# Layer 3 of a four-layer network: a quarter of B's products moved to GpSimd in half of the states, one ScalarE table for exp and ln, and a new schedule for a chunk's preparation

## The chip, the cores and the metric

The kernel runs on one core of a Trainium2 chip. A core has five engines with a queue each, which work side by side and wait for one another by semaphores: TensorE (in the profile PE; PEld is its weight load), VectorE (DVE), ScalarE (ACT), GpSimd (POOL) and SyncE (SP), which here only issues DMAs. The metric is the device time of one execution in microseconds, as the median of several.

## The reference

Four layers are applied one after the other to four images of 256 channels and 64 x 64 pixels, with a normalisation ahead of each: a deformable convolution (layer 0), an attention over all 4096 pixels (layer 1), a grouped deformable convolution (layer 2) and a selective state-space layer (layer 3, "mamba"). The change touches layer 3 only, which computes, for the L = 4096 pixels of an image in order:

```python
xz = einsum('bld,ed->ble', xs, in_proj_w)            # 256 -> 1024
u, res = split(xz, 2)                                 # 512 and 512 channels
u = silu(causal_conv4(u) + conv_b)
dt, Bm, Cm = split(u @ x_proj_w.T, [16, 32])          # 16, 16, 16
delta = softplus(dt @ dt_proj_w.T + dt_proj_b)        # 512 channels
state = exp(delta * A) * state + delta * Bm * u       # 512 x 16 states, along L
y = sum over the 16 states of state * Cm, + u * D
out = (y * silu(res)) @ out_proj_w.T
```

The state is a recurrence along the pixels; each of the 512 channels has 16 states, and A, Bm and Cm have one value for each of the 16.

## The kernel before

Channels lie on the 128 partitions, so 512 channels are 4 blocks of 128 (index `dc` in the code), and the pixels are cut into `NC` = 8 chunks of `C` = 512. For one image, layer 3 is a loop over 128 steps `s`: the chunk is `j = s // 16`, the state `n = s % 16`. A step does this for one state of one chunk:

- TensorE broadcasts row n of B to all partitions: a small bfloat16 matmul of `pick` with `bp` (three bfloat16 parts of B) into the one PSUM bank `bn` (L1419, in `state`).
- VectorE multiplies `du` (delta times u, 128 x 2048) by that row into the tile `h` (L1491).
- ScalarE forms `da` = exp(delta x A) block by block into two PSUM banks (L1498), and VectorE runs the recurrence over a block in place (L1499, a scan). So ScalarE can be at most two blocks ahead of VectorE.
- GpSimd keeps the last column as the start of the next chunk (`carry`, L1510) and multiplies `h` by row n of C (L1513). That row, `cn`, was broadcast to all partitions by a DMA from a small tensor `cd` in device memory (L1417, SP's queue).
- TensorE adds the four blocks of `h` of two steps ago to the four PSUM banks `y` by matmuls with the identity (L1411, in `add`). At n = 0 a matmul with a diagonal puts u x D there first (L1409). At n = 2 of the next chunk VectorE multiplies the finished y by the gate (L1468, `gated`).

A float32 matmul shows as two instructions (two passes) in the profile.

The order on TensorE, ScalarE, VectorE and GpSimd is written out by hand: each engine executes its instructions in program order. Between these instructions lies the preparation of the next chunk (`front(j)`): the normalised x (`begin`, L1245), four projections to u (L1213, copied by L1217), four convolutions of 8 passes (L1259, bias by L1264), the silu of u together with that of the last chunk's gate (L1273, L1229), the projection to dt, B and C (L1282, kept by L1286), the projection to delta with Abs and Relu (L1297, L1303, L1304), the parts of a softplus (Exp L1310, "+1" L1314, "1 - w" L1324, Ln L1326, and GpSimd's sums and products L1319, L1328 to L1330), the four gate projections (L1213 again), and the split of B into bfloat16 parts (`split`). `close(j)` projects a finished chunk to the output (L1369, L1373, copied by L1377 and sent by SP), fetches the next image's pixels and takes their statistics (`count`, L152).

Each piece has a place (step, half), and `LEAD` is how many steps ahead of its chunk the preparation begins, so that a piece of step k lies at state n = k - LEAD (negative: in the chunk before). `put(step, half, pe, rest)` enters a TensorE part and the rest. Half 0 lies between the second and the third scan, half 1 after the fourth, half 2 after the product with C, -1 after the product with B. `fill` issues the TensorE part early (that of half 0 at the end of the step before, that of half 1 ahead of the third scan), and `empty` issues the rest in its place. All these TensorE parts share one PSUM bank, "front", which is free again once ScalarE has read it.

In a step of before, TensorE's order is: the half-0 part, the half-1 part, `bn` of the next step, the eight passes of `add`. The code inserts a load of ScalarE's function table wherever the loaded set lacks the function; silu, exp and ln come from three sets, so a chunk has four loads.

## Time and profile before

| what | value |
|---|---|
| median of 3 runs | 9984.5 us (9975.76 to 9988.26) |
| the profiled execution's own time | 9981.35 us |
| its span, first to last instruction | 9979.5 us |
| granted TensorE clock, mean | 0.956 |
| layer 3's loop, first image | from 1571.69 us on, chunks of 123.08, 119.45, 119.45, 119.81, 119.45, 119.45, 118.95 us; the last to its last product 111.76 |
| the same, the other images | from 4045.13, 6517.47 and 8993.31 us on |
| a `cn` broadcast | 512 DMAs of 256 KB |

Times in the profile are in microseconds, those of single instructions in the groups in nanoseconds. A line of the groups gives: code line, engine, operation, output <- inputs with their shapes, number; then busy time in all and mean of one; then the engine's idle time just ahead of them, with what ended it. A line of a timeline gives start, length, engine, code line, operation and number of merged instructions, and in brackets how long the engine had been idle and what ended that.

### The profile page before, as it was taken

How to read it: one execution, taken by the hardware profiler on the slowest of the kernel's cores; microseconds unless marked ns; L12 is line 12 of the kernel's file. 1: busy time of each engine (PE TensorE's matmuls, PEld its weight loads, DVE VectorE, ACT ScalarE, POOL GpSimd, SP SyncE). 2: the span in 40 equal slices, each digit the busy share in tenths (PEclk: the TensorE clock that was granted, in tenths of full speed). 3: DMA queues.
4: the chain of work that ended last, by engine and by line, in shares of the span. 5: the costliest groups of instructions: out<-in, count | busy, mean ns of one | idle time of the engine just before them, and what ended most of it. 6: DMA issues, size and time to landing. Idle time of an engine off the chain costs nothing. (4 is left out here: it accounts for less than half of the span.)

```text
span 9979.5 us, 88756 instructions
## 1 busy us (share of the span) xinstructions
PE 8624.9 (86%) x29193; PEld 4231.9 (42%) x29193; DVE 7632.5 (76%) x8183; ACT 4959.9 (50%) x7576; POOL 6758.0 (68%) x3948
## 2 busy tenths in 40 slices
PE   5889998998778999899877899989977789998997
PEld 3643443333464344333346434433335643443333
DVE  4764597999676459899967646889996764679998
ACT  3743335665474332566557433266645733326664
POOL 3746786887574667688747467768875746777876
PEclk9999999999899999999989999999998999999999
DMA  7830011111793011111188201111118810111111
GB/s 264 319 138 1 31 48 38 46 45 49 258 329 113 1 34 52 36 46 45 44 293 324 82 1 40 48 40 44 45 42 313 322 63 1 42 52 34 40 41 33
DMA packets 377891, 956.56 MB, mean 96 GB/s; under 512 B 34675, under 2 KB 107820, under 8 KB 375372
## 3 DMA queue, kind: packets, MB, share of 16 engines
q0 software_dynamic: 165888, 604.05, 16.8%
q1 hardware_dynamic: 211532, 346.73, 11.1%
q8 instruction: 234, 3.83, 0.2%
q14 instruction: 237, 1.94, 0.1%
HBM read 784.59 MB, written 92.32 MB: 88 GB/s over the span
## 5 line engine op out<-in xcount | busy, mean ns | idle before, releaser
L1499 DVE TENSOR_TENSOR_SCAN h<-da,carry,h 128x512 f32<-128x512 f32 x2048 | 2470.5, 1264 | 138.3 <-ACT da L1498 89.7
L1513 POOL TENSOR_TENSOR h<-h,cn 128x2048 f32<-128x2048 f32 x508 | 2300.1, 4528 | 41.0 <-POOL carry L1510 0.2
L1498 ACT ACTIVATE da<-delta,l3a 128x512 f32<-128x512 f32 x2048 | 1389.1, 689 | 1138.6 <-DVE h L1499 1136.4
L1411 PE MATMUL y<-h,ident 128*128 128x512 f32 x4096 | 1930.8, 616 | 3.3 <-POOL h L1513 2.5
L344 POOL DMA_INDIRECT g<-tab,idx x1152 | 1355.1, 1176 | 756.7 <-issue 368.8
L565 POOL TENSOR_TENSOR acc<-acc,e 128x1024 f32<-128x1024 f32 x480 | 1125.2, 2344 | 541.6 <-ACT e L561 520.1
L388 PE MATMUL pz<-cols,l0w 128*128 128x256 f32 x4608 | 1216.2, 411 | 191.5 <-DVE cols L377 81.3
L1411 PEld LDWEIGHTS y<-h,ident 128*128 128x128 f32 x4096 | 809.8, 198 | 1295.1 <-issue 1233.3
L1491 DVE TENSOR_TENSOR h<-du,bn 128x2048 f32<-128x2048 f32 x512 | 1157.8, 2261 | 34.4 <-PE bn L1419 34.3
L353 DVE SCALAR_TENSOR_TENSOR r<-g,wx,r 128x512 f32<-128x512 f32 x1152 | 858.1, 745 | 368.2 <-ACT r L352 252.2
L462 DVE TENSOR_REDUCE m<-pm 128x3 f32<-128x1536 f32 (+2 forms) x340 | 599.3, 1763 | 699.7 <-PE pm L452 699.7
L388 PEld LDWEIGHTS pz<-cols,l0w 128*128 128x128 f32 x4608 | 896.4, 205 | 361.2 <-DVE cols L377 119.1
L561 ACT ACTIVATE e<-sc 128x1024 f32<-128x1024 f32 x512 | 496.0, 1020 | 1029.7 <-PE sc L548 1029.7
L572 PE MATMUL cx<-e,v 128*128 128x512 f32 x2048 | 1001.1, 616 | 0.0
L845 DVE TENSOR_TENSOR prod<-ring,A 128x1280 f32<-128x1280 f32 x640 | 922.6, 1480 | 79.1 <-DMA ring<-ring 60.8
L352 ACT ACTIVATE r<-g,wx 128x512 f32<-128x512 f32 x1152 | 826.4, 717 | 258.9 <-DMA g<-tab,idx 212.9
L862 PE MATMUL pacc<-prod,ident 128*128 128x512 f32 x1920 | 912.9, 609 | 35.3 <-DVE prod L845 23.3
L854 POOL TENSOR_TENSOR prod<-prod 128x512 f32<-128x512 f32 x640 | 800.1, 1274 | 184.2 <-DVE prod L845 161.6
L370 PE MATMUL pt<-ident,acc 128*128 128x128 f32 x2304 | 426.7, 294 | 297.2 <-DVE acc L361 232.9
L1510 POOL COPY carry<-h 128x4 f32<-128x4 f32 x512 | 98.0, 191 | 804.6 <-DVE h L1499 793.0
L572 PEld LDWEIGHTS cx<-e,v 128*128 128x128 f32 x2048 | 352.4, 189 | 599.1 <-issue 596.6
L360 ACT ACTIVATE acc<-r,wy 128x256 f32<-128x256 f32 x1152 | 571.9, 496 | 24.6 <-DVE r L353 22.1
(254 smaller groups left out, 10959.9 us busy)
## 6 DMA issues: line engine op xcount, KB each, us to landing
cn<-cd SPq DMA_DIRECT2D x512, 256.0 KB
tab<-vt SPq DMA_DIRECT2D x112, 640.0 KB
ring<-ring SPq DMA_DIRECT2D x288, 126.0 KB
ring<-ring SPq DMA_DIRECT2D x288, 124.0 KB
g<-tab,idx POOLq DMA_INDIRECT x1152
x<-in_x SPq DMA_DIRECT2D x64, 256.0 KB
out<-x SPq DMA_DIRECT2D x56, 256.0 KB
l0w<-in_l0w SPq DMA_DIRECT2D x4, 2304.0 KB
```

Of the source, the lines that this page charges most:

```text
L344: nc.gpsimd.indirect_dma_start(out=g[:], out_offset=None, in_=tab[:, :], in_offset=bass.IndirectOffsetOnAxis(ap=idx[:, t, k : k + 1], axis=0),
L353: nc.vector.scalar_tensor_tensor(r, g[:, :, 1, :], wx[:, 1, t, k : k + 1], r, ALU.mult, ALU.add)
L388: nc.tensor.matmul(sums[m][:, ot, :256], wf[:, i, bass.ts(ot, P)], cols[m][:, i, :], start=(i == 0), stop=(i == 17),)
L565: nc.gpsimd.tensor_add(b["acc"], b["acc"], e)
L572: nc.tensor.matmul(blocks[qb]["cx"], v[:, 4 * (i + kt // 4 * 4) + kt % 4, :], e[:, bass.ts(i % 2, 512)], start=(kt == 0 and i == 0), stop= ...
L845: nc.vector.tensor_mul(d["prod"][:, :, t, :].rearrange("p x (g c) -> p x g c", c=GC), ring[y // VR % 4][:, :, y % VR, :].rearrange("p x (g ...
L862: nc.tensor.matmul(d["pd"], self.ident, prod[:, wx, :], start=(wy == 0 and wx == 4), stop=(wy == WIN - 1 and wx == 2),)
L1411: nc.tensor.matmul(c["ys"][dc], self.ident, h[:, dc, :], start=False, stop=(n == DS - 1))
L1491: nc.vector.tensor_mul(h, c["du"], c.pop(("bn", n)).to_broadcast([P, 4, C]))
L1498: nc.scalar.activation(da, c["delta"][:, dc, :], AF.Exp, scale=al[:, dc, n : n + 1])
L1499: nc.vector.tensor_tensor_scan(h[:, dc, :], da, h[:, dc, :], carry[:, dc, n : n + 1], ALU.mult, ALU.add)
L1513: nc.gpsimd.tensor_mul(h, h, cn.to_broadcast([P, 4, C]))
```

## The change

1. **B's products.** In the states 14, 15, 0, 1, 2, 3, 4 and 5 (`helped`) VectorE multiplies three of the four blocks of `du`; GpSimd multiplies the fourth into a tile `hq` (two buffers) in the step before (`quarter(s + 1)`, between the second and the third scan), and the fourth scan reads `hq`. [...]its row of B is broadcast by a DMA into `bs` (two buffers), from `cd`, which now holds C and B. `ahead` issues both broadcasts two steps ahead; `cn` has four buffers in place of six.
2. **Order.** `bn` of the next step is issued right after the second scan, ahead of the half-1 part. At n = 2 VectorE's product of step 3 is issued there too, between the second and the third scan, ahead of `empty(s, 0)` with the silu.
3. **One table.** `tables()` loads the set that has both exp and ln after the silus, so that neither Ln nor the exp after it needs a load.
4. **The preparation.** `LEAD` becomes 5 (3 in place of 2 for the first). Projections to u go to n = 11, 12, 13 and 15, all in half 1 (they were at 12/1, 13/0, 13/1 and 14/0); convolutions to 13/0, 14/1, 0/1 and 1/1 (14/1, 15/1, 0/1, 1/1); "1 - w" from 8/0 to 8/1; the gates from 10/0 to 11/1 to 9/0 to 10/1; the output projections from 7/1 and 9/1 to 6/1 and 7/1; the statistics for most chunks from n = 9 to n = 2, half 0. The silu stays at 2/0, the shares at 3/1, delta at 4 and 5, Exp at 6/0, Ln at 9/0, and GpSimd's sums where they were.
5. **Tiles.** `kept` takes the buffer of `xn3`; `tiny`, whose exp loaded a table in `first`, goes.

```diff
-        NC, LEAD = N // C, 4
+        NC, LEAD = N // C, 5
...
-            kept = pa.tile([P, 2, C], F32, tag="kept", name="kept")
-            tiny = pa.tile([P, 1], F32, tag="tiny", name="tiny")
...
+            def tables():
+
+                nc.scalar.preload_act_table_set("natural_log_exp_and_others")
...
-                nc.scalar.activation(tiny, self.eps, AF.Exp)
+                tables()
...
-                c["cd"] = self.dram.tile([DS, C], F32, tag="cd", name="cd")
-                nc.sync.dma_start(out=c["cd"], in_=dbc[16:32, :])
+                c["cd"] = self.dram.tile([2 * DS, C], F32, tag="cd", name="cd")
+                nc.sync.dma_start(out=c["cd"], in_=dbc[16:48, :])
...
-                    put((dc + 1) // 2, (dc + 1) % 2, *project(j, dc, lambda dc=dc: c["up"][:, dc, 3:]))
+                    put(
+                        (0, 1, 2, 4)[dc], 1, *project(j, dc, lambda dc=dc: c["up"][:, dc, 3:])
+                    )
...
-                    put(2 + dc, 1, *convolve(dc))
+                    put((2, 3, 5, 6)[dc], dc > 0, *convolve(dc))
+
                 def silu():
                     nc.scalar.activation(c["u"], c["u"], AF.Silu)
                     gate_silu(j - 1)
-
-                put(6, 0, None, silu)
+                    tables()
+
+                put(7, 0, None, silu)
...
-                put(7, 1, shares, keep)
+                put(8, 1, shares, keep)
...
-                    put(8 + dc // 2, dc % 2, *step(dc))
-                put(10, 0, None, lambda: nc.scalar.activation(c["du"], c["du"], AF.Exp, scale=-1.0))
+                    put(9 + dc // 2, dc % 2, *step(dc))
+                put(11, 0, None, lambda: nc.scalar.activation(c["du"], c["du"], AF.Exp, scale=-1.0))
...
                 put(
-                    12,
-                    0,
+                    13,
+                    1,
                     None,
                     lambda: nc.scalar.activation(c["du"], c["w"], AF.Identity, bias=self.ones[:, 0:1], scale=-1.0),
                 )
-                put(13, 0, None, lambda: nc.scalar.activation(c["w"], c["w"], AF.Ln))
-                last = 17 if j > 1 else 15
...
+                put(14, 0, None, lambda: nc.scalar.activation(c["w"], c["w"], AF.Ln))
+                last = 18 if j > 1 else 16
...
-                    at = ((14, 0), (14, 1), (15, 0), (15, 1)) if j > 1 else ((10, 1), (11, 0), (11, 1), (12, 1))
+                    at = ((14, 0), (14, 1), (15, 0), (15, 1)) if j > 1 else ((11, 1), (12, 0), (12, 1), (13, 1))
                     put(*at[dc], *gate(j, dc))
...
-                    todo.append((11 + 2 * ot - LEAD, 1, *project(ot)))
+                    todo.append((6 + ot, 1, *project(ot)))
...
-                    todo.append((13 - LEAD + DS if j < NC - 2 else 17 - LEAD, -1, None, lambda: count(j)))
+                    todo.append((2 + DS, 0, None, lambda: count(j)) if j < NC - 2 else (13, -1, None, lambda: count(j)))
...
-            def state(j, n):
-
-                c = chunks[j]
-                cn = c["cn", n] = pb.tile([P, 1, C], F32, tag="cn", name="cn", bufs=6)
-                nc.sync.dma_start(out=cn, in_=c["cd"][n : n + 1, :].unsqueeze(0).to_broadcast([P, 1, C]))
-                bn = c["bn", n] = pbb.tile([P, 1, C], F32, tag="bn", name="bn")
-                nc.tensor.matmul(bn[:, 0, :], pick[:, n, :], c["bp"], start=True, stop=True)
+
+            hs, helped = {}, (14, 15, 0, 1, 2, 3, 4, 5)
+
+            def ahead(s):
+
+                if s < NC * DS:
+                    j, n = s // DS, s % DS
+                    c = chunks[j]
+                    for name, r, bufs in (("cn", n, 4), ("bs", DS + n, 2)):
+                        if name == "cn" or n in helped:
+                            t = c[name, n] = pb.tile([P, 1, C], F32, tag=name, name=name, bufs=bufs)
+                            nc.sync.dma_start(
+                                out=t, in_=c["cd"][r : r + 1, :].unsqueeze(0).to_broadcast([P, 1, C])
+                            )
+
+            def state(s):
+
+                if s < NC * DS:
+                    c = chunks[s // DS]
+                    bn = c["bn", s % DS] = pbb.tile([P, 1, C], F32, tag="bn", name="bn")
+                    nc.tensor.matmul(bn[:, 0, :], pick[:, s % DS, :], c["bp"], start=True, stop=True)
+
+            def quarter(s):
+
+                if s < NC * DS and s % DS in helped:
+                    c = chunks[s // DS]
+                    hq = hs[s, 3] = pb.tile([P, C], F32, tag="hq", name="hq")
+                    nc.gpsimd.tensor_mul(hq, c["du"][:, 3, :], c.pop(("bs", s % DS))[:, 0, :])
+
+            def product(s):
+
+                if s not in hs:
+                    c, n = chunks[s // DS], s % DS
+                    h = hs[s] = pb.tile([P, 4, C], F32, tag="h", name="h", bufs=4)
+                    d = 3 if n in helped else 4
+                    nc.vector.tensor_mul(h[:, :d, :], c["du"][:, :d, :], c.pop(("bn", n)).to_broadcast([P, d, C]))
...
-                    at = DS * (j - 1) - (LEAD if j > 1 else 2) + step
+                    at = DS * (j - 1) - (LEAD if j > 1 else 3) + step
...
-                    h = pb.tile([P, 4, C], F32, tag="h", name="h", bufs=4)
-                    nc.vector.tensor_mul(h, c["du"], c.pop(("bn", n)).to_broadcast([P, 4, C]))
+                    product(s)
+                    h = hs[s]
+                    ahead(s + 2)
...
+                        hb = hs.pop((s, dc), h[:, dc, :])
                         nc.vector.tensor_tensor_scan(
-                            h[:, dc, :], da, h[:, dc, :], carry[:, dc, n : n + 1], ALU.mult, ALU.add
+                            h[:, dc, :], da, hb, carry[:, dc, n : n + 1], ALU.mult, ALU.add
                         )
...
                     scan(0)
                     scan(1)
+                    quarter(s + 1)
+                    state(s + 1)
+                    if n == 2:
+                        product(s + 1)
                     empty(s, 0)
                     fill(s, 1)
...
-                    if s + 1 < total:
-                        state((s + 1) // DS, (s + 1) % DS)
```

More of the change, by code (lines that the diff above doesn't have):

```diff
@@ L1264, in rest @@
                         nc.scalar.activation(c["u"][:, dc, :], c["b"], AF.Identity, bias=cb[:, dc : dc + 1])
-                        if dc == 0:
+                        if dc == 2:
                             nc.gpsimd.tensor_copy(tail, c["up"][:, :, C : C + 3])
@@ L1286, in keep @@
                     nc.scalar.copy(c["dbc"], c["b"])
-                    c["cd"] = self.dram.tile([DS, C], F32, tag="cd", name="cd")
-                    nc.sync.dma_start(out=c["cd"], in_=c["dbc"][16:32, :])
-                put(7, 1, shares, keep)
+                    c["cd"] = self.dram.tile([2 * DS, C], F32, tag="cd", name="cd")
+                    nc.sync.dma_start(out=c["cd"], in_=c["dbc"][16:48, :])
+                put(8, 1, shares, keep)
                 def step(dc):
@@ L1314, in one @@
                     nc.scalar.activation(c["w"], c["du"], AF.Identity, bias=self.ones[:, 0:1])
-                put(10, 1, None, one)
-                put(10, 2, None, lambda: nc.gpsimd.tensor_add(c["delta"], c["delta"], c["du"]))
-                put(
-                    12,
-                    0,
+                put(11, 1, None, one)
+                put(11, 2, None, lambda: nc.gpsimd.tensor_add(c["delta"], c["delta"], c["du"]))
+                put(
+                    13,
+                    1,
                     None,
@@ L1325, in front @@
                 )
-                put(13, 0, None, lambda: nc.scalar.activation(c["w"], c["w"], AF.Ln))
-                last = 17 if j > 1 else 15
-                put(13, 2, None, lambda: nc.gpsimd.tensor_add(c["delta"], c["delta"], c["du"]))
-                put((13 + last) // 2, 2, None, lambda: nc.gpsimd.tensor_add(c["delta"], c["delta"], c["w"]))
+                put(14, 0, None, lambda: nc.scalar.activation(c["w"], c["w"], AF.Ln))
+                last = 18 if j > 1 else 16
+                put(14, 2, None, lambda: nc.gpsimd.tensor_add(c["delta"], c["delta"], c["du"]))
+                put((14 + last) // 2, 2, None, lambda: nc.gpsimd.tensor_add(c["delta"], c["delta"], c["w"]))
                 put(last, 2, None, lambda: nc.gpsimd.tensor_mul(c["du"], c["delta"], c["u"]))
                 for dc in range(4):
-                    at = ((14, 0), (14, 1), (15, 0), (15, 1)) if j > 1 else ((10, 1), (11, 0), (11, 1), (12, 1))
+                    at = ((14, 0), (14, 1), (15, 0), (15, 1)) if j > 1 else ((11, 1), (12, 0), (12, 1), (13, 1))
                     put(*at[dc], *gate(j, dc))
@@ L1354, in front @@
                 for i in range(3):
-                    put((11, 12, 14)[i], i % 2, None, split(i))
+                    put((12, 13, 15)[i], i % 2, None, split(i))
                 return todo
@@ L1371, in pe @@
                             )
-                        xs = kept[:, ot, :] if last else x[:, ot, bass.ts(j, C)]
+                        xs = c["kept"][:, ot, :] if last else x[:, ot, bass.ts(j, C)]
                         nc.tensor.matmul(c["b"], self.ident, xs, start=False, stop=True)
                     def rest():
-                        to = kept if last else x[:, :, bass.ts(j, C)]
+                        to = c["kept"] if last else x[:, :, bass.ts(j, C)]
                         nc.scalar.copy(to[:, ot, :], c["z", ot])
@@ L1382, in close @@
                 for ot in range(2):
-                    todo.append((11 + 2 * ot - LEAD, 1, *project(ot)))
+                    todo.append((6 + ot, 1, *project(ot)))
                 if not last:
-                    todo.append((15 - LEAD, -1, None, lambda: fetch(j)))
-                    todo.append((13 - LEAD + DS if j < NC - 2 else 17 - LEAD, -1, None, lambda: count(j)))
+                    todo.append((10, -1, None, lambda: fetch(j)))
+                    todo.append((2 + DS, 0, None, lambda: count(j)) if j < NC - 2 else (13, -1, None, lambda: count(j)))
                 return todo
@@ L1400, in keep @@
             def keep():
+                kept = chunks[-1]["kept"] = pa.tile([P, 2, C], F32, tag="xn3", name="kept")
                 for ct in range(2):
@@ L1435, in layer3 @@
             slots.setdefault((last, 0), []).append((None, keep))
-            slots.setdefault((last + 2, 0), []).append((None, lambda: gate_silu(NC - 1)))
+            slots.setdefault((last + 2, 0), []).append((None, lambda: (gate_silu(NC - 1), tables())))
             slots.setdefault((last + 2, -1), []).append((None, lambda: fetch(NC - 1)))
@@ L1482, in layer3 @@
                     rest()
-                state(0, 0)
+                for s in range(2):
+                    ahead(s)
+                state(0)
+                quarter(0)
                 fill(0, 0)
```

## The prediction

> **What bounds the kernel now.** I read the page's engine shares and costliest groups first, then the loop of layer 3 alone by windows, then VectorE's timeline there, gap by gap, then ScalarE's and TensorE's timelines around each gap.
>
> ```profile
> PE 8624.9 (86%) x29193; PEld 4231.9 (42%) x29193; DVE 7632.5 (76%) x8183; ACT 4959.9 (50%) x7576; POOL 6758.0 (68%) x3948
> ...
> L1499 DVE TENSOR_TENSOR_SCAN h<-da,carry,h 128x512 f32<-128x512 f32 x2048 | 2470.5, 1264 | 138.3 <-ACT da L1498 89.7
> L1513 POOL TENSOR_TENSOR h<-h,cn 128x2048 f32<-128x2048 f32 x508 | 2300.1, 4528 | 41.0 <-POOL carry L1510 0.2
> L1498 ACT ACTIVATE da<-delta,l3a 128x512 f32<-128x512 f32 x2048 | 1389.1, 689 | 1138.6 <-DVE h L1499 1136.4
> ...
> L1491 DVE TENSOR_TENSOR h<-du,bn 128x2048 f32<-128x2048 f32 x512 | 1157.8, 2261 | 34.4 <-PE bn L1419 34.3
> ```
>
> Over the whole span no engine stands out; the change touches layer 3 only, so the window of one of its chunks counts (columns: length, then busy us of PE, PEld, DVE, ACT, POOL, then granted clock):
>
> ```profile
> 1931.00:2051.00 120.00, 108.84 (x254) 46.46 (x253) 115.78 (x87) 76.77 (x104) 96.07 (x41) 0.99 0.16 44
> ```
>
> VectorE is busy 96% of it, TensorE 91%, GpSimd 80%. VectorE's product L1491 and four scans L1499 follow each other at 2.37 + 4 x 1.18 = 7.09 us a step. From first product to first product a chunk takes 119.45 us: 16 x 7.09 = 113.44, the gating of the last chunk's y at n = 2 with 2.30, and waits (or statistics lying in one of them) of some 3.7. They are these, in chunk 1 of the first image:
>
> ```profile
> 1717.56 2.46 DVE L1499 TENSOR_TENSOR_SCAN h<-da,carry,h 128x512 f32<-128x512 f32 x2 [1.59 <-ACT da L1498]
> ...
> 1768.81 2.46 DVE L1499 TENSOR_TENSOR_SCAN h<-da,carry,h 128x512 f32<-128x512 f32 x2 [1.25 <-ACT da L1498]
> ...
> 1807.10 2.29 DVE L1491 TENSOR_TENSOR h<-du,bn 128x2048 f32<-128x2048 f32 x1 [0.39 <-PE bn L1419]
> ```
>
> The first is the silu (n = 2), the second the Ln (n = 9), the third TensorE late (n = 15); 0.17 more falls at n = 8. Behind the second stands ScalarE's queue:
>
> ```profile
> 1757.75 2.00 ACT L1324 ACTIVATE du<-w,ones 128x2048 f32<-128x2048 f32 x1 [1.57 <-POOL delta L1319]
> ...
> 1762.24 1.31 ACT L1498 ACTIVATE da<-delta,l3a 128x512 f32<-128x512 f32 x2
> 1763.57 1.28 ACT L1326 ACT_TABLE_LOAD   x1
> 1764.86 1.91 ACT L1326 ACTIVATE w<-w 128x2048 f32<-128x2048 f32 x1
> 1766.79 1.28 ACT L1498 ACT_TABLE_LOAD   x1
> 1768.09 1.30 ACT L1498 ACTIVATE da<-delta,l3a 128x512 f32<-128x512 f32 x2
> ```
>
> **GpSimd's quarter.** In 8 of 16 states VectorE multiplies 3 of 4 blocks. Its 128x1024 product took 1.225 us (L1515), the 128x2048 one 2.261: 1.01 ns an element, so a quarter less is 0.525 us, and a step is 6.57. Per chunk 8 x 0.525 = 4.2 us. GpSimd gets eight 128x512 products; the nearest row is its 64x512 subtraction at 1.16 us, so about 1.2 each, 9.6 a chunk: 96 becomes 106 of some 118. In its order the quarter stands before the product with C; it is tightest after the long du product (n = 13), where I get quarter 15 done 3.9 us into its step, with its scan due at 5.4. Two more broadcasts wait on SP's queue, 256 KB each, eight a chunk; the DMA share is 0.16 and they leave a step ahead: nothing. Of cn's buffers four are left; cn of s+2 waits for the product of s-2, over two steps before need: nothing.
>
> [...]512 products stayed within 2257 to 2289 ns beside a GpSimd busy most of the time. I take 4.2.
>
> **One table for exp and ln.** Two of four loads a chunk go, both at the Ln: 2 x 1.28 = 2.57 us of ScalarE, on VectorE's path only if its wait at n = 9 goes. It doesn't, for the Identity L1324 moves from n = 8, half 0, to half 1, just ahead of that queue. From the end of the last exp of step 8 ScalarE must then do Identity 2.0, two casts 1.25, two exps 1.3, Ln 1.91, the gate's copy 0.59 (moved there too) and an exp 0.69 = 7.7 us; before it was 1.25 + 1.3 + 2.57 + 1.91 + 0.65 = 7.7. VectorE again waits 1.6 (with 0.1 at the first scan). Its own earlier wait of 0.17 goes.
>
> **The product amid the silu.** At n = 2 ScalarE has two loads and two silus, 6.4 us. VectorE now has the product of step 3 (1.84) and, for three images, two statistics (1.25) to do there. The wait of 1.59 becomes 0; the statistics, hidden in the Ln's wait before, show as 1.25 (without them the same time is lost to TensorE's diagonal and shares products before n = 4).
>
> **The preparation dealt anew.** TensorE's float32 passes follow at 0.43 us. A chunk has 236 of these and 16 of bn at 0.21: 105 us, so it fits into 118. But bn of s+1 now comes first in its step and can't start until VectorE's product has read the one bank (2.32 us in); then the half-1 work, eight adds (3.44), and the half-0 work of the next step. There is one "front" bank, and whatever stands in half 0 delays ScalarE's third exp, due 4.7 us in. I walked the step times on:
> - n = 4: dtw's product ends at 2.5, Abs and Relu at 3.8, exp at 4.5, due at 4.2: 0.36; at n = 5 another 0.12.
> - n = 9 to 10: gate 0's copy is behind the Ln (5.55 us into step 9), so gate 1 can't start before, TensorE stands idle 3 us, the adds end 2.1 into step 10, gate 2 at 4.0; copy, cast and exp end at 5.9: 1.25.
> - n = 13: bn at 2.32, project 1.72, adds 3.44 end 0.6 into step 13, the first convolution (8 passes) at 4.2; bias and exp end at 5.6: 0.97.
> - n = 15: the 0.39 goes; 0 to 0.4 is the bound.
>
> [...]
>
> ```profile
> 1743.51 0.38 PE L1419 MATMUL bn<-bp,pickn 128*128 128x512 bf16 x1 [2.46 <-DVE h L1491]
> 1743.72 3.59 PE L1411 MATMUL y<-h,ident 128*128 128x512 f32 x8
> ...
> 1757.69 0.38 PE L1419 MATMUL bn<-bp,pickn 128*128 128x512 bf16 x1 [2.43 <-DVE h L1491]
> 1757.90 5.29 PE L1411 MATMUL y<-h,ident 128*128 128x512 f32 x8
> ```
>
> After one idle of 2.4 us the eight passes took 3.59 us, after another 5.29, at a granted clock of 0.60 to 0.78. [...]Halved, gate 1 and all behind it come 1.7 later. I count half, 0.85, and keep 0 and 1.7.
>
> **The sum for a chunk.** 8 x 7.09 + 8 x 6.57 = 109.2; gating 2.25; n = 2: 1.25; n = 4, 5: 0.48; n = 9: 1.6; n = 10: 1.25 + 0.85; n = 13: 0.97. Together 117.9, [...]against 119.45: 1.57 us less, 37.7 over the 24 chunks with a chunk before and after them. The last chunk of an image has no preparation: 4.2 x 4 = 16.8. The first chunk gains 3.7 of its 4.2 (no early product at its silu, n = 4, whose wait of 3.31 grows by 0.5), but a convolution of 8 passes is moved ahead of the first bn (3.4 and a copy's wait, 4.2 in all), and the next chunk's xn (1.5) falls behind the Ln; its other waits shrink: together 0, between -4 and +4 an image. Total 54.5 us. The profiled execution took 9981.35 (span 9979.5), so 9926.9; the median of the runs, 9984.5, lies 3.1 above it, and from it I get 9930.
>
> **Rivals.**
> *The waits at n = 10 and 13 don't come*, TensorE being early enough. For it speaks that 13 us a chunk are free on TensorE, against it that bn's one bank ties it to VectorE's product. A chunk is then 109.2 + 2.25 + 1.25 + 0.48 + 1.6 = 114.8: 24 x 4.64 + 16.8 = 128, 9856.
> *No difference.* The cut is given back wholly: waits of some 2.3 us a chunk beyond mine, as when the slow clock falls on n = 10 and half of it on n = 13 in all chunks. 9965 to 10,004.
> *Slower: TensorE's clock.* Its place is n = 9 to 13: [...]It decides from 24x = 24 x 2.42 + 17, x = 3.1 us a chunk over the warm 117.0; [...]For it: 5.29 against 3.59. Against: most gaps left are shorter than those that cooled it.
> *The table doesn't hold*: if Ln and exp kept loading their own, 2.57 us would be added at n = 9 in 28 chunks, 72 us, 10,002.
>
> **How the numbers follow.** My forecast, 9905 to 9960, has 0.50, the missing waits 0.27, no difference 0.10, slower by the clock 0.10, the table 0.03. A change within 0.2% (20 us) can't be told from none in this kernel. Faster by more 0.77, within 0.10, slower 0.13. The range runs from the missing waits, 9845, to 9975, a little into no difference; left out are the slower cases and most of the unchanged.
>
> **What would show it.** L1491's successor with 128x1536 outputs 256 times at about 1.74 us; new GpSimd products of 128x512, 256 times at about 1.2, none of whose scans waits; table loads on ScalarE in layer 3 down from four to two a chunk; no wait at n = 2 beyond 0.3; waits of VectorE on da at n = 9 (1.6), 10 (1.25 or 2.95), 13 (1.0); chunks of 117 to 118.7 us. I am wrong if waits on da at n = 10 and 13 are missing, or if a wait on hq or on bn of over 1 us a chunk appears.

## The result and the profile after

| | before | after |
|---|---|---|
| median, side by side (7 runs each) | 9981.96 us (9969.87 to 9988.26) | 9952.22 us (9939.75 to 9967.15) |
| ratio, with its 95% interval | | 0.9972 (0.996 to 0.9983) |
| profiled execution, and its span | 9981.35, 9979.5 | 9953.54, 9951.7 |
| granted TensorE clock, mean | 0.956 | 0.952 |

The changed kernel is faster by 29.7 us in the medians and by 27.8 in the profiled executions. The forecast was 9930 with 9905 to 9960 as the likeliest case's own range, so the outcome is that case by its number. But 54.5 us were to be gained, and about half of that came: a sum with the right sign in which two terms were wrong in opposite directions.

Lines of the page of after (share and busy time of the engines, then the costliest groups):

```profile
PE 8629.7 (87%) x29193; PEld 4253.8 (43%) x29193; DVE 7497.1 (75%) x8183; ACT 4866.0 (49%) x7508; POOL 7067.5 (71%) x4204
...
L1543 DVE TENSOR_TENSOR_SCAN h<-da,carry,h 128x512 f32<-128x512 f32 x1792 | 2173.5, 1265 | 225.4 <-ACT da L1541 179.8
L1561 POOL TENSOR_TENSOR h<-h,cn 128x2048 f32<-128x2048 f32 x508 | 2300.4, 4528 | 41.3 <-POOL carry L1558 0.6
...
L1458 DVE TENSOR_TENSOR h<-du,bn 128x2048 f32<-128x2048 f32 (+1 forms) x512 | 1020.5, 1993 | 39.9 <-PE bn L1443 39.9
```

VectorE has 135 us less to do, 137 of it in the product (1157.8 before, 1020.5 after), and GpSimd 310 more. But the scan's idle time behind ScalarE's `da` has grown, from 89.7 us over all scans to 179.8 over those that read `h`. The window that was shown of before, 1931 to 2051 us (length; busy us of PE, PEld, DVE, ACT, POOL; clock), reads now:

```profile
1931.00:2051.00 120.00, 110.70 (x258) 47.33 (x257) 113.20 (x89) 74.93 (x104) 107.48 (x49) 0.99 0.23 63
```

GpSimd went from 96 to 107 of 120 us, as worked out. The whole loop of layer 3 can be cut at VectorE's products. Added over the four images, from the first product to the last, with VectorE's wait ahead of the first one beside it:

| mean us | before | after | times | change in all |
|---|---|---|---|---|
| wait ahead of the first product | 5.7 | 9.0 | 4 | +13.3 |
| first chunk of an image | 123.40 | 129.93 | 4 | +26.1 |
| middle chunk | 119.40 | 116.72 | 24 | -64.2 |
| last chunk | 110.96 | 109.43 | 4 | -6.1 |
| sum | 3825.7 | 3794.9 | | -30.9 |

This sum over the loop agrees with the 27.8 us of the profiled executions, so the rest of the kernel matters for 3 us at most. Below, "the loop" always means it: 3825.7 before, 3794.9 after.

**A middle chunk.** VectorE's timeline in one (third image; start, length, what; in brackets the idle time ahead and who ended it), states 9, 10 and 13, then 2 of the next chunk:

```profile
6824.98 2.46 DVE L1543 TENSOR_TENSOR_SCAN h<-da,carry,h 128x512 f32<-128x512 f32 x2 [1.15 <-ACT da L1541]
...
6833.55 2.46 DVE L1543 TENSOR_TENSOR_SCAN h<-da,carry,h 128x512 f32<-128x512 f32 x2 [1.37 <-ACT da L1541]
...
6855.63 2.46 DVE L1543 TENSOR_TENSOR_SCAN h<-da,carry,h 128x512 f32<-128x512 f32 x2 [0.71 <-ACT da L1541]
...
6890.63 1.73 DVE L1458 TENSOR_TENSOR h<-du,bn 128x1536 f32<-128x1536 f32 x1
6892.27 1.28 DVE L152 BATCH_NORM_STATS2 st<-x 128x6 f32<-128x512 f32 x2
```

The three waits stand where they were forecast, and the silu's wait at n = 2 (1.59 before) is gone here, filled by the early product and the statistics; in 9 of the 24 middle chunks 0.41 to 0.81 us of it is left. The wait at n = 10 has two main sizes. Around gate 1, ScalarE and TensorE in this chunk, then TensorE and VectorE two chunks later:

```profile
6823.78 0.57 ACT L1221 COPY sres<-front 128x512 f32<-128x512 f32 x1
...
6824.40 1.98 PE L1217 MATMUL front<-xn,l3a 128*128 128x512 f32 x4 [2.76 <-ACT sres L1221]
...
6826.22 3.60 PE L1421 MATMUL y<-h,ident 128*128 128x512 f32 x8
```

```profile
7056.65 2.42 PE L1217 MATMUL front<-xn,l3a 128*128 128x512 f32 x4 [2.76 <-ACT sres L1221]
7058.87 4.90 PE L1421 MATMUL y<-h,ident 128*128 128x512 f32 x8
```

```profile
7067.49 2.46 DVE L1543 TENSOR_TENSOR_SCAN h<-da,carry,h 128x512 f32<-128x512 f32 x2 [3.07 <-ACT da L1541]
```

Both times TensorE stood idle for 2.76 us until gate 0's copy. Once gate 1's four passes took 1.98 us and the eight behind them 3.60, once 2.42 and 4.90, and VectorE's wait is 1.37 or 3.07, 1.70 longer. The granted clock over these twelve passes (the third number from the end; behind it the DMA's share and rate) was 1.00 and 0.76:

```profile
6824.40:6829.90 5.50, 5.50 (x13) 2.58 (x14) 4.82 (x4) 2.94 (x5) 4.69 (x3) 1.00 0.31 95
7056.60:7063.80 7.20, 7.15 (x13) 3.17 (x14) 6.47 (x5) 2.99 (x5) 6.37 (x3) 0.76 0.28 73
```

Below, "cold" means this: TensorE at the lower granted clock. In 11 of the 24 middle chunks the wait was 2.76 or more (once 4.41), in the other 13 it was 1.37 or 1.38.

**The first chunk.** The same image: first product, then state 3 and the silu at state 4:

```profile
6506.92 1.75 DVE L1458 TENSOR_TENSOR h<-du,bn 128x1536 f32<-128x1536 f32 x1 [8.00 <-PE bn L1443]
...
6539.24 2.46 DVE L1543 TENSOR_TENSOR_SCAN h<-da,carry,h 128x512 f32<-128x512 f32 x2 [2.98 <-ACT da L1541]
6546.87 1.28 DVE L1543 TENSOR_TENSOR_SCAN h<-da,carry,h 128x512 f32<-128x512 f32 x1 [5.18 <-ACT da L1541]
```

```profile
6521.87 0.38 PE L1443 MATMUL bn<-bp,pickn 128*128 128x512 bf16 x1 [2.77 <-DVE h L1458]
6522.09 5.29 PE L1265 MATMUL front<-up,conv 128*128 128x512 f32 x8
...
6534.08 0.38 PE L1443 MATMUL bn<-bp,pickn 128*128 128x512 bf16 x1
6534.30 3.60 PE L1265 MATMUL front<-up,conv 128*128 128x512 f32 x8
```

```profile
6537.93 0.69 ACT L1270 ACTIVATE u<-front,l3b 128x512 f32<-128x512 f32 x1 [6.03 <-PE front L1265]
```

At state 4, where before had one wait of 3.31, VectorE waits 2.98 and 5.18 for `da` and 0.97 for `bn`. The line of before, same image:

```profile
6554.35 2.46 DVE L1499 TENSOR_TENSOR_SCAN h<-da,carry,h 128x512 f32<-128x512 f32 x2 [3.31 <-ACT da L1498]
```

In state 2 TensorE stands idle 2.77 us until VectorE's product has read `bn`, then does a convolution cold (5.29 us at a granted clock of 0.68, in place of 3.60 at 1.00 in state 3). From there to the second `bn` shown it is busy without a gap, so in state 3 it is still late by all of that: the last convolution begins only at 6534.30, its result keeps ScalarE waiting for 6.03 us, and only behind that come an exp and the two silus.

With this order the silu's wait is handed on. `bn` of state 6 waits for VectorE's product of state 5, the eight passes of the shares stand behind it and run cold (6.03 us at a granted clock of 0.59), and VectorE waits 0.75 and 2.46 for `da` at state 6 (means of the four first chunks), where before had none:

```profile
6551.02 0.58 PE L1443 MATMUL bn<-bp,pickn 128*128 128x512 bf16 x1 [6.05 <-DVE h L1458]
6551.41 6.03 PE L1290 MATMUL front<-u,l3b 128*128 128x512 f32 x8
```

And at state 15 the fourth scan waits for GpSimd's quarter:

```profile
6635.22 1.28 DVE L1543 TENSOR_TENSOR_SCAN h<-da,carry,hq 128x512 f32<-128x512 f32 x1 [2.64 <-POOL hq L1450]
```

In this chunk GpSimd runs its last three sums and products of the preparation (4.5 us each) while VectorE is in states 12, 13 and 15, in a middle chunk of the same image in 10, 12 and 14. It has no gap between the first and the third, and the quarter stands right behind the third. All waits of a first chunk together are 21.6 us in place of 10.7, and the products only 4.2 shorter.

**The last chunk** has no preparation, but the output projections are there (TensorE, ScalarE, VectorE):

```profile
7383.55 0.59 PE L1443 MATMUL bn<-bp,pickn 128*128 128x512 bf16 x1 [4.28 <-DVE h L1458]
7383.93 6.19 PE L1378 MATMUL front<-sres,l3b 128*128 128x512 f32 x8
```

```profile
7392.23 4.81 DVE L1543 TENSOR_TENSOR_SCAN h<-da,carry,h 128x512 f32<-128x512 f32 x4 [1.65 <-ACT da L1541]
```

With little else to do TensorE waits 4.28 us for VectorE's product, is cold in the projection's eight passes (6.19 us at a granted clock of 0.58), and ScalarE's exps wait behind the copy of their result. Before, the projection stood ahead of `bn` and ran at a granted clock of 1.00 (3.60 us), and VectorE had no such wait in the last chunk:

```profile
7422.52 3.60 PE L1369 MATMUL front<-sres,l3b 128*128 128x512 f32 x8
```

### The profile page after: what moved, and what is told of

The parts are those of the page before. It is cut to its first block, busy times and chain, and to the rows that moved or that the text cites. A ratio compares the mean times of both kernels' runs of the same rounds, so it can differ in the third digit from the quotient of the medians.

```text
span 9951.7 us, 89396 instructions
## 1 busy us (share of the span) xinstructions
PE 8629.7 (87%) x29193; PEld 4253.8 (43%) x29193; DVE 7497.1 (75%) x8183; ACT 4866.0 (49%) x7508; POOL 7067.5 (71%) x4204
## 3 DMA queue, kind: packets, MB, share of 16 engines
q14 instruction: 243, 1.98, 0.1%
## 5 line engine op out<-in xcount | busy, mean ns | idle before, releaser
L1543 DVE TENSOR_TENSOR_SCAN h<-da,carry,h 128x512 f32<-128x512 f32 x1792 | 2173.5, 1265 | 225.4 <-ACT da L1541 179.8
L1421 PE MATMUL y<-h,ident 128*128 128x512 f32 x4096 | 1885.1, 604 | 11.3 <-POOL h L1561 11.3
L1458 DVE TENSOR_TENSOR h<-du,bn 128x2048 f32<-128x2048 f32 (+1 forms) x512 | 1020.5, 1993 | 39.9 <-PE bn L1443 39.9
L1217 PE MATMUL front<-xn,l3a 128*128 128x512 f32 x896 | 461.5, 639 | 118.9 <-ACT sres L1221 79.7
```

The source lines that it names most:

```text
L1421: nc.tensor.matmul(c["ys"][dc], self.ident, h[:, dc, :], start=False, stop=(n == DS - 1))
L1458: nc.vector.tensor_mul(h[:, :d, :], c["du"][:, :d, :], c.pop(("bn", n)).to_broadcast([P, d, C]))
L1543: nc.vector.tensor_tensor_scan(h[:, dc, :], da, hb, carry[:, dc, n : n + 1], ALU.mult, ALU.add)
```

## The experiments

Runs differ by tens of us in layers that no edit touches: the kernel before took 9981.96, 10,003.64, 10,011.47 and 10,021.01 us beside the four groups of runs, and outside the loop the traces below hold between 6154 and 6195 us. So what a run shows is read from the loop in its trace, one trace for each kernel, and the whole time stands beside it with that of the kernel before in the same group. Middle chunks that an edit leaves as they were came out up to 0.33 us apart (116.72 and 116.39), so less than that is not read as an effect. The loop of all runs, in us:

| run | whole time | before in its group | wait ahead of the first product, sum | first chunk | middle | last | loop |
| --- | --- | --- | --- | --- | --- | --- | --- |
| before | 9981.35 | - | 22.8 | 123.40 | 119.40 | 110.96 | 3825.7 |
| after | 9953.54 | 9981.96 | 36.1 | 129.93 | 116.72 | 109.43 | 3794.9 |
| quarter alone | 9953.99 | 10,011.47 | 18.5 | 123.29 | 117.64 | 107.24 | 3764.1 |
| after, no quarter | 10,085.75 | 10,003.64 | 36.2 | 130.87 | 120.52 | 112.96 | 3904.0 |
| after, tables as before | 10,054.72 | 10,003.64 | 37.2 | 133.15 | 119.68 | 108.15 | 3874.7 |
| after, no early product | 10,076.07 | 10,003.64 | 32.0 | 129.49 | 120.98 | 108.52 | 3887.5 |
| after, gates later | 9924.47 | 10,011.47 | 36.3 | 130.00 | 114.34 | 108.66 | 3735.1 |
| after, first chunk's old places | 9932.29 | 10,011.47 | 14.2 | 127.91 | 116.39 | 108.72 | 3754.1 |
| after, bn in its old order | 9975.44 | 10,011.47 | 36.2 | 126.54 | 117.31 | 107.31 | 3787.1 |
| combination | 9844.34, median of 4 | 10,003.64 | 14.2 | 118.78 | 114.03 | 107.31 | 3655.4 |
| the same, no early product in the first chunk | 9858.07 | 10,021.01 | 14.2 | 121.66 | 113.80 | 107.20 | 3661.0 |
| the same, bn early in the first chunk | 9841.87 | 10,021.01 | 14.2 | 123.04 | 113.96 | 107.30 | 3670.6 |

The questions were: why the first chunk lost where nothing was to change; what each part is worth alone; and whether the waits at n = 10 and in the last chunk are what they were taken for.

### The quarter alone, on the kernel before

GpSimd's products of a block, their broadcasts, and the tiles that make room for them, and nothing else:

```diff
+            hs, helped = {}, (14, 15, 0, 1, 2, 3, 4, 5)
...
-                    nc.vector.tensor_mul(h, c["du"], c.pop(("bn", n)).to_broadcast([P, 4, C]))
+                    d = 3 if n in helped else 4
+                    nc.vector.tensor_mul(h[:, :d, :], c["du"][:, :d, :], c.pop(("bn", n)).to_broadcast([P, d, C]))
+                    ahead(s + 2)
...
                     scan(1)
+                    quarter(s + 1)
                     empty(s, 0)
```

> The kernel before, with GpSimd's quarter alone (same states, same tiles, bs two steps ahead, no early product, four table loads, the old places and the old order). Theory A (VectorE sets the pace and the old waits stay as they are): each chunk 4.2 us shorter, middle chunks 115.2, 134 us less than before in all, better than the changed kernel by about 90. Theory B (with shorter steps the old places leave TensorE late): waits on bn at n = 14 to 3 take 2 us a chunk or more, middle chunks 117 to 118, 50 to 70 us less than before.

The loop fell by 61.7 us, twice what the whole change gave (4 of these lie in the wait ahead of the first product, which this edit doesn't touch). The last chunk gained 3.7 of the 4.2 us of shorter products, the middle chunk only 1.8, the first nothing. Where the 4.2 go in a middle chunk, VectorE's timeline of this run shows at states 1, 2, 2 and 15:

```profile
1704.55 1.76 DVE L1513 TENSOR_TENSOR h<-du,bn 128x1536 f32<-128x1536 f32 x1 [0.42 <-PE bn L1421]
1711.63 1.75 DVE L1513 TENSOR_TENSOR h<-du,bn 128x1536 f32<-128x1536 f32 x1 [0.42 <-PE bn L1421]
1720.35 1.28 DVE L1522 TENSOR_TENSOR_SCAN h<-da,carry,h 128x512 f32<-128x512 f32 x1 [2.21 <-ACT da L1521]
...
1808.26 1.75 DVE L1513 TENSOR_TENSOR h<-du,bn 128x1536 f32<-128x1536 f32 x1 [0.84 <-PE bn L1421]
```

In the states with the shorter step, `bn` comes too late by 0.42 (n = 0, 1, 2) and 0.84 (n = 15): in the old order it stands behind both pieces of the preparation, so TensorE's queue sets the step. And the silu's wait rises from 1.59 to 2.21.

### The change without the quarter

```diff
-            hs, helped = {}, (14, 15, 0, 1, 2, 3, 4, 5)
+            hs, helped = {}, ()
```

> The changed kernel without GpSimd's quarter: VectorE multiplies all four blocks in all states; all else as changed. Theory A (VectorE sets the pace in the new order, its waits stay): 4.2 us more in each chunk, middle chunks 120.9, 134 us more than the changed kernel in all. Theory B (a part of the quarter only becomes waits in the changed kernel, in the first chunk above all, where TensorE is late): middle chunks about 120.5, but first chunks longer by at most 1 and last chunks by 2 to 3; some 100 us more.

A middle chunk takes 3.8 us longer, nearly the 4.2 of the term "8 x 0.525", and the last 3.5. The first chunk takes 0.9 more: there something else sets the end. Two facts follow. Within the new schedule the quarter is worth 109 us, against 62 within the old one. And the new schedule without the quarter is 78 us slower than before (3904.0 against 3825.7; whole times 10,085.75 against 10,003.64 on the same chip). Of these 78 us, 43 fall ahead of and in the first chunk, 27 in the middle chunks and 8 in the last. Taken together, the order, the table and the places are no gain of their own.

### The change with the table loads of before

`tables()` does nothing, so Ln and the exp behind it load their own sets:

```diff
-                nc.scalar.preload_act_table_set("natural_log_exp_and_others")
+                pass
```

> The changed kernel without the call for the one table, so that Ln and the exp after it load their own as before: four loads a chunk. Theory A (my reckoning: ScalarE's queue at the Ln sets the wait there, so that both loads come in full): 2 x 1.28 = 2.57 us more of wait at n = 9 in 24 middle chunks and at n = 11 in the first ones, 72 us more in all, and more where it delays the gates. Theory B (the loads are hidden): under 15 us.

ScalarE at n = 9, and VectorE behind it:

```profile
1782.46 1.28 ACT L1334 ACT_TABLE_LOAD   x1
1783.75 1.91 ACT L1334 ACTIVATE w<-w 128x2048 f32<-128x2048 f32 x1
1786.15 1.28 ACT L1541 ACT_TABLE_LOAD   x1
1787.45 1.30 ACT L1541 ACTIVATE da<-delta,l3a 128x512 f32<-128x512 f32 x2
```

```profile
1788.17 2.46 DVE L1543 TENSOR_TENSOR_SCAN h<-da,carry,h 128x512 f32<-128x512 f32 x2 [3.85 <-ACT da L1541]
```

The wait is 3.85 in place of 1.15, 2.70 more for the two loads, and the middle chunk is 2.96 longer; the loop is 80 us longer. With "1 - w" moved to just ahead of this queue, the saving was needed to keep the wait where it had been, as the prediction had argued, and it bought no time beyond that.

### The change without the early product at the silu

```diff
-                    if n == 2:
-                        product(s + 1)
```

> The changed kernel without the early product at n = 2. Theory A (it fills the silu's wait): a wait on da of 1 to 2.2 us comes back at n = 2, middle chunks 1 to 1.8 us longer, 24 to 43 us in all; first chunks unchanged, within 1 us, since their silu is at n = 4. Theory B (the early product moves TensorE's lateness about): first chunks shorter by 2 us or more without it.

The loop is 93 us longer, all of it in the middle chunks (+4.3 each). At n = 2 and 4 VectorE waits 1.4 and 1.8 us on the average, and the wait at n = 10 is 2.98 or more in 23 of 24 chunks, where it had been 2.76 or more in 11 of 24. Neither theory had allowed for the last two, and a middle chunk lost more than twice what was expected:

```profile
1793.83 2.46 DVE L1543 TENSOR_TENSOR_SCAN h<-da,carry,h 128x512 f32<-128x512 f32 x2 [3.07 <-ACT da L1541]
```

In this chunk ScalarE's copy of gate 1 begins 3.76 us behind the end of gate 0's (1786.70 against 1782.94), in place of 2.07 in the changed kernel's chunk with the wait of 1.37. So the slow gate 1, which came in 11 of 24 chunks there, came in nearly all here, and the edit touches nothing between gate 0 and gate 1.

### The gates half a step later

Gates 0 to 3 of a middle chunk from 9/0, 9/1, 10/0, 10/1 to 9/1, 10/0, 10/1, 11/0, so that gate 0's copy isn't behind the Ln and gate 1 isn't late for n = 10:

```diff
-                    at = ((14, 0), (14, 1), (15, 0), (15, 1)) if j > 1 else ((11, 1), (12, 0), (12, 1), (13, 1))
+                    at = ((14, 1), (15, 0), (15, 1), (16, 0)) if j > 1 else ((11, 1), (12, 0), (12, 1), (13, 1))
```

> The changed kernel, with the four gate projections half a step later (n = 9/1, 10/0, 10/1, 11/0 in place of 9/0 to 10/1), so that none stands behind the Ln. Theory A (the copy of gate 0 behind the Ln holds the one front bank and makes the waits of n = 10): the waits on da at n = 10 (2.14 us on average in the middle chunks) go, those of n = 9 fall from 1.27 to about 0.7, 0.5 comes at n = 11, where the xn stands, and 0.3 at n = 13: 1.9 us a middle chunk, 46 us in all. Theory B (TensorE is simply short of time there): the waits only move to n = 11 to 13, and nothing is gained.

VectorE's timeline, all its waits of over 0.2 us from n = 9 to 13 in one middle chunk:

```profile
1778.85 2.46 DVE L1543 TENSOR_TENSOR_SCAN h<-da,carry,h 128x512 f32<-128x512 f32 x2 [0.67 <-ACT da L1541]
1793.43 2.46 DVE L1543 TENSOR_TENSOR_SCAN h<-da,carry,h 128x512 f32<-128x512 f32 x2 [0.29 <-ACT da L1541]
1808.42 2.46 DVE L1543 TENSOR_TENSOR_SCAN h<-da,carry,h 128x512 f32<-128x512 f32 x2 [0.70 <-ACT da L1541]
```

The wait at n = 10 is gone in all chunks, that at n = 9 fell from 1.15 to 0.67, the one at n = 13 stayed. A middle chunk takes 114.34 us, 2.4 less, the loop 59.7 less. This confirms the mechanism of n = 10: a copy behind the Ln, TensorE idle, gate 1 late and, in 11 of 24 chunks, cold, gate 2 in half 0 of the next step.

### The first chunk's pieces in their old places

```diff
-                        (0, 1, 2, 4)[dc], 1, *project(j, dc, lambda dc=dc: c["up"][:, dc, 3:])
+                        *(((0, 1), (1, 1), (2, 1), (4, 1)) if j > 1 else ((1, 1), (2, 0), (2, 1), (3, 0)))[dc], *project(j, dc, lambda dc=dc: c["up"][:, dc, 3:])
...
-                    put((2, 3, 5, 6)[dc], dc > 0, *convolve(dc))
+                    put(*((((2, 0), (3, 1), (5, 1), (6, 1)) if j > 1 else ((3, 1), (4, 1), (5, 1), (6, 1)))[dc]), *convolve(dc))
...
-                    1,
+                    1 if j > 1 else 0,
```

> The changed kernel, with the pieces of the first chunk's preparation (j = 1) back in their old places: no convolution ahead of the first bn, the fourth projection at n = 0, half 0, the convolutions at 0/1 to 3/1, '1 - w' in half 0. In the changed kernel the first product of the four images waits 36.1 us in all (22.8 before) and the first chunks take 130.2, 130.5, 129.5, 129.5 us (123.1, 124.5, 123.0, 123.1 before). Theory A (the convolution costs only the start; the chunk itself is slow because bn now comes first on TensorE): the start goes back to about 23, the first chunks stay at 128 to 131; in all 13 us less. Theory B (the places are what makes the first chunk slow): the first chunks go back to about 121 to 124 as well; in all 35 to 45 us less.

The last two lines put "1 - w" back into half 0. The wait ahead of the first product falls from 8.00 (12.06 in the first image) to 3.56 in all images. The convolution that the change had put ahead of the first `bn` is 4.44 of that in each image; the other 4.06 us of the first image are projections that ran cold there (twice four passes in 3.78 us at a granted clock of 0.50, in place of 1.98 at 1.00 in the third image), as they also did in two images of before (3.75 to 3.78 us at 0.50 to 0.52; the wait was 7.8 in place of 3.56). The first chunk itself only fell by 2.0, as much as its wait at n = 11 behind "1 - w" (2.69 to 0.71). Its waits at n = 4 were the same to the hundredth, 2.98 and 5.18 for `da`, 0.97 for `bn`. So with `bn` early the places cost the start, and not the silu.

### bn in its old order, but for n = 2

```diff
-                    state(s + 1)
                     if n == 2:
+                        state(s + 1)
                         product(s + 1)
...
                     empty(s, 2)
+                    if n != 2:
+                        state(s + 1)
```

> The changed kernel, with bn of the next step back at the end of a step's TensorE work (behind the half-1 part, ahead of the adds), but for n = 2, where the early product needs it. Theory A (bn first makes TensorE wait for VectorE's product and cools it): first chunks from 130 to 122 to 125 us, last chunks from 110.5 to about 107.6, the waits on da at n = 10 smaller; 30 to 50 us less in all. Theory B (bn first is needed, since the shorter steps leave TensorE late): waits on bn of 0.5 to 1 us in several of n = 13 to 3, middle chunks from 116.7 to 118 or more, 30 us or more slower in the middle chunks.

The last chunk takes 107.31, as with the quarter alone, with no wait at n = 7 and 8 and no projection pass of over 0.70 us (1.06 in the changed kernel): this part of the loss is the order of `bn`. The first chunk gained 3.4, since the waits at n = 6, 3.2 us, are gone: the shares stand ahead of `bn` again. But its two waits at n = 4 (4.41 for `bn`, 4.41 for `da`) add up to 8.8, against 9.1. On those the run is no test, because its exception for n = 2 holds in the first chunk too, and there `bn` stands ahead of a convolution (third image):

```profile
6547.82 0.58 PE L1443 MATMUL bn<-bp,pickn 128*128 128x512 bf16 x1 [6.18 <-DVE h L1458]
6548.20 4.88 PE L1265 MATMUL front<-up,conv 128*128 128x512 f32 x8
```

A middle chunk lost 0.6: VectorE waits 0.98 for `bn` at n = 10, while the wait at n = 13 is gone. With the gates where they are, the early `bn` is right for the middle chunks, and it is wrong for the last.

### The combination

The gates later; the old places for the first chunk; `bn` early only in the middle chunks and around an early product; the first chunk's early product at n = 4, where its silu is; and for later chunks the third projection at 13/0 and the first convolution at 13/1 (they were 13/1 and 13/0), so that no piece of 8 passes stands in half 0 of n = 13:

```diff
-                        (0, 1, 2, 4)[dc], 1, *project(j, dc, lambda dc=dc: c["up"][:, dc, 3:])
+                        *(((0, 1), (1, 1), (2, 0), (4, 1)) if j > 1 else ((1, 1), (2, 0), (2, 1), (3, 0)))[dc], *project(j, dc, lambda dc=dc: c["up"][:, dc, 3:])
...
-                    put((2, 3, 5, 6)[dc], dc > 0, *convolve(dc))
+                    put((2 if j > 1 else 3, 3 if j > 1 else 4, 5, 6)[dc], 1, *convolve(dc))
...
-                    state(s + 1)
-                    if n == 2:
+                    early = 0 < j < NC - 1 or s in (4, last + 2)
+                    if early:
+                        state(s + 1)
+                    if s == 4 or j and n == 2:
                         product(s + 1)
...
+                    if not early:
+                        state(s + 1)
```

> The changed kernel with (1) the gates half a step later, (2) the third projection at n = 13, half 0, and the first convolution in half 1, (3) the first chunk's pieces in their old places, (4) the early product of the first chunk at its own silu, n = 4, and (5) bn in its old order in the first and the last chunk. Theory A (the waits found so far are separate and come from these places): middle chunks 113.7 us (114.4 with the gates alone, less the 0.7 at n = 13), first chunks 122 to 126, last ones 108, the start 14 to 23 us in all; 90 to 110 us less than the changed kernel, about 9850. Theory B (they are one shortage of TensorE, which only moves): middle chunks stay over 114.3, under 75 us less.

Measured: 9844.34 us (9837.33 to 9851.33) against 10,003.64 for the kernel before on the same chip, ratio 0.9836 (0.9819 to 0.9852). The loop is 139.5 us shorter than that of the changed kernel, 170.3 shorter than before. First chunks take 118.78, middle chunks 114.03 (the wait at n = 13 is gone), last chunks 107.31. It is faster than the kernel before; the changed kernel did not run beside it, and against that the loop decides.

### Two parts of the combination taken back in the first chunk

No early product at n = 4:

```diff
-                    if s == 4 or j and n == 2:
+                    if j and n == 2:
```

> The combination run without VectorE's early product at the first chunk's silu (n = 4). In the combination the first chunks took 118.7 us, against 130 in the changed kernel, and VectorE waited 0.39 for bn at n = 4 and 2.76 for da at n = 5. Theory A, the silu of the first chunk needs work beside it: without the early product VectorE waits some 3.3 for da at n = 4, as in the kernel before, of which only part is taken from the 2.76 at n = 5, and the first chunks take 119.7 to 121 us. Theory B, the wait is only moved from n = 5 to n = 4: 118.4 to 119.2. The middle chunks stay at 114.0 and the first products wait 3.56 in either case.

And the early `bn` in the first chunk:

```diff
-                    early = 0 < j < NC - 1 or s in (4, last + 2)
+                    early = j < NC - 1 or s == last + 2
```

> The combination run with the changed kernel's order of bn (right after the second scan) in the first chunk too; its pieces keep the places of before and the early product at n = 4 stays. Theory A, the order of bn is what made the first chunks long, because TensorE waits there for VectorE's product and cools, while the preparation of two chunks lies behind it: 123 to 127 us instead of 118.7, with waits on da at n = 4 to 6 of 5 us or more in all and the eight passes of a convolution at 5.29 us in place of 3.60. Theory B, the places and the early product are what matters: 118 to 119.5 us. The middle chunks stay at 114.0.

The first chunks took 121.66 and 123.04, in place of 118.78. The whole times can't tell these kernels apart, but the first chunks can: the four of a run lie within 1.6 us, and those of different runs don't overlap. The combination has 2.76 us of waiting for `da` and 0.39 for `bn` at n = 4. Without the early product it is 4.41 and 0.39, and the chunk is a little longer than either theory had it. With the early `bn` VectorE waits 0.97 for `bn`, 2.98 and 3.53 for `da`. The chain in the third image, first in the combination: TensorE in state 2, with VectorE's product of that state, then ScalarE's copy of the last convolution:

```profile
6477.59 3.70 PE L1265 MATMUL front<-up,conv 128*128 128x512 f32 x8 [1.26 <-ACT u L1270]
6481.13 0.38 PE L1443 MATMUL bn<-bp,pickn 128*128 128x512 bf16 x1
```

```profile
6478.47 1.73 DVE L1458 TENSOR_TENSOR h<-du,bn 128x1536 f32<-128x1536 f32 x1
```

```profile
6491.84 0.69 ACT L1270 ACTIVATE u<-front,l3b 128x512 f32<-128x512 f32 x1 [1.80 <-PE front L1265]
```

The same with the early `bn`:

```profile
6465.48 0.59 PE L1443 MATMUL bn<-bp,pickn 128*128 128x512 bf16 x1 [2.75 <-DVE h L1458]
6465.86 4.86 PE L1265 MATMUL front<-up,conv 128*128 128x512 f32 x8
```

```profile
6463.70 1.73 DVE L1458 TENSOR_TENSOR h<-du,bn 128x1536 f32<-128x1536 f32 x1
```

```profile
6481.28 0.69 ACT L1270 ACTIVATE u<-front,l3b 128x512 f32<-128x512 f32 x1 [6.00 <-PE front L1265]
```

In the combination the convolution begins 0.88 us ahead of VectorE's product (6477.59 against 6478.47) and `bn` waits behind it. With `bn` first it begins 2.16 behind the product (6465.86 against 6463.70), 3.0 later, after an idle of 2.75, and takes 4.86 in place of 3.70, 1.2 more. That is 4.2 together, and the first chunk is 4.3 longer. So TensorE gives the time up in two ways at once: it waits, and its passes are slower after the wait. The copy shows the delay: ScalarE stood idle 6.00 us for it, in place of 1.80.

From the changed kernel's 129.93 to the combination's 118.78 the first chunk's steps are therefore: places 2.0 (old places), `bn`'s order and the rest 6.3 (127.91 to 121.66), the early product 2.9. The middle one also holds the later chunk's pieces at n = 13 and the later gates; the gates alone did nothing to the first chunk (130.00), and the run with the early `bn` gives 4.3 for the order alone. How the remaining 2 us divide was not tried, and the parts depend on the order in which they are taken: in the changed kernel, `bn`'s order (but for n = 2) gave 3.4.

## Why the prediction was right, and where it was not

**The number: right in part by luck.** Against the forecast the first chunks, with the wait ahead of them, lost 39.4 us and the last ones 10.7, and the middle chunks gained 26.5 more than foreseen. Either miss alone would have put the forecast's 9930 at about 9980 or 9904, outside 9905 to 9960.

**The middle chunk: right in kind, too small a gain.** Forecast 117.9, measured 116.72; a gain of 2.68 us in place of 1.57. Term by term: the quarter's 4.2 came (3.8 by the run without it), with products of 1.73 us for 1.74 and GpSimd's at 1.28 for 1.2. GpSimd's quarters did not slow VectorE's products: all 256 took 1.72 to 1.76 us beside a GpSimd that is busy 90% of the time. n = 2: the statistics exposed with 1.28, as said, and 0.20 of waiting on the average where none was expected. "n = 4, 5: 0.48": 0.04. n = 9: 1.6 forecast, 1.31 measured. n = 10: 1.25 + 0.85 forecast, 2.14 measured, with 1.37 and 3.07 for the two cases 1.25 and 2.95; the weight of one half for the slow clock met 11 of 24. n = 13: 0.97 forecast, 0.59 measured (0.70 in 20 of 24 chunks). n = 15: gone. Together these terms are 0.9 us a chunk below the forecast, some 21 of the 26.5 us by which the middle chunks' gain was forecast too small.

**The clock: the rows were right to be heard.** Behind two idles of nearly one length, 2.46 and 2.43 us, before had eight passes in 3.59 and in 5.29 us (granted clock 1.00 and 0.68), and the prediction counted the slow case half. Gate 1 was slow, after 2.76 us, in 11 of 24 chunks, at a price of 1.70 us for a counted 1.7. Taking that idle for safe would have missed about 0.8 us a chunk.

**The first chunk: the step that failed.** "Its other waits shrink: together 0, between -4 and +4 an image." To come to 0, its own terms (+3.7, -4.2, -1.5) needed 2.0 us from these waits, and no line was given for it. Measured is a loss of 9.9 an image: 3.3 ahead of the first product and 6.5 in the chunk. The first is the convolution, charged with 4.2 and measured with 4.44 at the same clock (before had cold projections in two images, after in one). The second is the failure: the waits didn't shrink but grew, to 9.1 at n = 4 in place of 3.31, and to 3.2 at n = 6 in place of none. The prediction had walked the middle chunk's steps with `bn` first and saw at n = 10 and 13 what it does to a piece behind it; for the first chunk it only added up the moved pieces and didn't walk the steps again. Taken alone, in the combination, the early `bn` costs the first chunk 4.3 us, 3.0 of waiting and 1.2 of slower passes; the early product that its silu lacks is worth 2.9 more. "None of whose scans waits" was wrong there too: at n = 15 of the first chunk the fourth scan waits 1.0 to 2.6 us for `hq`, which is one of the prediction's own signs of being wrong. In all other chunks no scan does. In the combination's first chunks it is still 2.0 on the average; no run tried to remove it.

**The last chunk: mis-sized.** "The last chunk has no preparation: 4.2." It gained 1.5. The output projections, which are there, were moved and then stood behind `bn` on a TensorE that had waited 4.28 us; with `bn` in its old order the chunk gained 3.7. Both failures have one root: an order and places chosen for the middle chunks were costed step by step only in them.

**The table: right.** In a middle chunk no gain beyond keeping the wait at n = 9, and 2.7 us there if the loads come back. **The rivals:** the missing waits didn't come by the change itself, though the later gates nearly give that case (114.34 against 114.8); the slow clock's case needed 3.1 us a chunk, and at gate 1 it cost 1.70 in 11 of 24, 0.8 on the average.

## What to carry to other kernels

When the order of one engine's queue is changed for the steady state, the first and the last turn of the loop have to be walked again step by step: here the middle gained 64 us and the ends gave 33 of it back. An instruction that waits for another engine, put early in an in-order queue, delays whatever is behind it (by 3.0 us in the combination's first chunk), and on TensorE that work was slower too (4.86 us in place of 3.70); where the queue has work that is due, the wait belongs behind that work. And before several edits are bundled, ask for each what it is worth without the others: the quarter alone gave twice what the bundle gave, and the bundle's other parts cost 78 us without it.

## What the runs showed that was not expected

The same idle of TensorE, 2.76 us ahead of gate 1, left the next passes fast in 13 chunks (gate 1's four in 1.98 us, the eight behind them in 3.60) and cold in 11 (the twelve together in 7.0 to 8.7 us in place of 5.6). The mean granted clock over a chunk hardly shows it, 0.99 in the window above; over these passes alone it is 1.00 in the 13 and 0.64 to 0.79 in the 11.

The granted clock has two values in the changed kernel's trace, 1 and 0.5. The length of the idle doesn't say which of the two the next passes get, and what does was not shown. In the run without the early product the wait at n = 10 was the long one, 2.98 or more, in 23 of 24 chunks. A schedule with such an idle ahead of a piece on the path has two durations here: behind it VectorE waited 1.37 or 1.38 us in the one case and 2.76 or more in the other.
